# A last batch of graphs: update's start, block sums and message additions put in another order

## The chip, the cores and the metric

The kernel runs on one core of one Trainium2 chip. The time is device microseconds of that core, as the median of several runs. It was 2236.86 us before the change (three runs, 2236.06 to 2238.81). A profiled execution of 2235.71 us, with a span of 2233.9 us, gives the trace.

## The reference

There are 64 graphs of 256 nodes with 256 features each (fp32), and a 256 x 256 adjacency per graph. Two layers follow one another:

```python
# layer 0, per graph
h = relu(bn(conv1(x)));  x_conv = relu(bn(conv2_17taps(h)) + x)
s = x @ w_se.T + b_se                         # 3 numbers per node
A = exp(-(|s_n|^2 + |s_m|^2 - 2 s_n.s_m)) * adj
x_nmp = A @ relu(x @ w_msg.T + b_msg)
gi = concat(x_conv, x_nmp) @ w_ih.T + b_ih;  gh = x @ w_hh.T + b_hh
r = sigmoid(gi_r + gh_r);  z = sigmoid(gi_z + gh_z)
n = tanh(gi_n + r * gh_n)
x = layernorm(x + (1 - z) * n + z * x)
# layer 1
h = layernorm(x)
x = layernorm(x + x + relu((adj @ h) @ W_rel + b_rel + h @ W_root))
```

## The kernel before, in words

The graphs are worked in eight batches of eight. The 17-tap convolution of a batch is computed for the batch ahead, in a transformed form, while the graphs of the present batch go through the gates. In the last batch (`first_k` = 56 to graph 62) no convolution is left to run beside them, so that batch has a loop of its own (L1246 to L1277). Graph 63 is done by `last_graph`.

Every engine works its instructions in the order in which the program issues them; `manual_schedule` keeps that order for all five. So the order of the calls in the loop is the order on each engine. Several functions are generators: each `step(...)` issues the instructions up to the next `yield`. A pass of graph k works on five graphs at once:

- `load(k + 3)`, `load_x(k + 1)`: SP's DMAs of the transposed x, the adjacency and x.
- `block_gates(k)`, four steps (`ga`): the gates of graph k as a block product with seven products of left and right sums, TensorE (PE) into four PSUM banks `ps_a`, `ps_d`, `ps_b`, `ps_c`. VectorE (DVE) adds each product into its place in `XF` (`onto`, L831). The third step accumulates a further product into `ps_a` with `start=False`; it may start only when DVE has read the first product there. The fourth step makes the n part of `gh` (`ps_n`, L856; DVE's addition at L858).
- `block_sums(k + 1, i)`: four DVE additions (L808 to L811) that make left sums of one input of the next graph: i = 0 its transposed x, 1 its message result (`NMP`), 2 its convolution (`xc`).
- `passing(k + 1)`: PE's product of masked weights and messages; ACT copies it to `NMP` (L738).
- `factors(k + 2)`, `distances(k + 2)`, `mask(k + 2)`: the exponentials and the masking of a graph's weights. `distances` has four small PE matmuls (L724) and two exponentials on ACT (L726); `mask` is one DVE product (L729).
- `messages(k + 3)`, two steps (`msg`): PE's product into `ps_msg` (L678); then DVE's additions (L688 and L690 twice), ACT's relu (L692) and five small GpSimd (POOL) operations (L696 to L700).
- `update(k)`, three steps (`up`): first two DVE operations on `nn` and tanh on ACT (L873); then `w` (L877 to L879), its statistics (L864, L865 twice), and on POOL the powers for the layer norms (L886 to L888) and a shift (L890, L891); then `h` on DVE (L896) and x1 on ACT (L899).
- `transposes_h(k - 1)`, `project(k - 1)`, `aggregate(k - 1)`: layer 1 of the graph before: PE's transposes (L909), ACT's `hT` (L911), PE's product with both weights (L922), ACT's copies of one half to `hr` (L923), PE's product with the adjacency (L934), DVE's `y` (L936, L938), its statistics, POOL's powers, and ACT's last scaling (L950) with the output DMA (L951).

One place of `block_gates`, in its third step:

```python
t = product(a, 5, False)
onto(0, 1, t, 1)
onto(1, 0, t, 0)
onto(0, 1, product(b_, 2, False))
squash(0)
```

Of the kernel before, what the change touches and what calls it, by code (L numbers as in the profile page):

```python
# [17 lines left out]
B, N, D = 64, 256, 256  # L18
# [58 lines left out]
def gnn_two_layers(  # L77
# [22 lines left out]
    def bank(name):  # L100
        return psum.tile([P, 512], F32, tag="ps", name=name)
# [548 lines left out]
    def load(k):  # L650

        if k >= B:
            return
        load_xt(k)
        load_adj(k)
# [9 lines left out]
    def load_x(k):  # L665
        if k < B:
            XG[k] = work.tile([P, C, D], F32, tag="x", name="x")
            nc.sync.dma_start(out=XG[k], in_=x[k].rearrange("(c p) d -> p c d", p=P))
# [39 lines left out]
    def factors(k):  # L708
        st, ns = ST[k]
        ps = bank("ps_sT")  # L710
        for m in range(C):
            nc.tensor.transpose(ps[:ROWS, m * P:(m + 1) * P], st[:, m, :ROWS], ident)
        lr = ahead.tile([ROWS, 2, N], F32, tag="lr", name="lr", bufs=1)
        nc.scalar.activation(lr[:, 0, :], ps[:ROWS, :N], AF.Identity, bias=lone[:, 1:2], scale=lone[:, 0:1])
        nc.scalar.copy(lr[:, 1, :], ps[:ROWS, :N])
        ST[k] = (lr, ns)

    def distances(k):
        lr, ns = ST[k]
        AT[k] = ahead.tile([P, C, N], F32, tag="AT", name="AT", bufs=2)  # L720
        pss = [bank("ps_dist") for _ in range(C)]
        for m in range(C):
            r = slice(m * SR, m * SR + 4)
            nc.tensor.matmul(pss[m][:, :N], lr[r, 0, m * P:(m + 1) * P], lr[r, 1, :], start=True, stop=True)  # L724
        for m in range(C):
            nc.scalar.activation(AT[k][:, m, :], pss[m][:, :N], AF.Exp, bias=ns[:, m:m + 1], scale=2.0)  # L726

    def mask(k):
        nc.vector.tensor_mul(AT[k], AT[k], ADJ[k])  # L729

    def passing(k):
        NMP[k] = work.tile([P, C, N], F32, tag="nmp", name="nmp")
        ps = bank("ps_nmp")
        for d in range(C):
            for m in range(C):
                nc.tensor.matmul(ps[:, d * N:(d + 1) * N], MSG[k][:, m, d * P:(d + 1) * P], AT[k][:, m, :],  # L736
                                 start=(m == 0), stop=(m == C - 1))
        nc.scalar.copy(NMP[k].rearrange("p c n -> p (c n)"), ps)  # L738
# [59 lines left out]
    def block_sums(k, i):  # L798

        if i == 2:  # L800
            xc, g = XC[k]
            v = xc[:, :, g, :]
        else:
            v = (XT, NMP)[i][k]
        a11, a12, a21, a22 = (v[:, c, n * P:(n + 1) * P] for n in range(C) for c in range(C))
        at = S * D + ((k % 2) * 3 + i) * 4 * P
        s1, s2, s3, s4 = (XF[:, at + j * P:at + (j + 1) * P] for j in range(4))
        nc.vector.tensor_add(s1, a21, a22)  # L808
        nc.vector.tensor_sub(s2, s1, a11)
        nc.vector.tensor_sub(s3, a11, a21)  # L810
        nc.vector.tensor_sub(s4, a12, s2)  # L811
        LEFT[k, i] = (a11, a12, s4, a22, s1, s2, s3)
# [54 lines left out]
    def update(k):  # L867

        rz, gn = RZ[k]
        nn = work.tile([P, C, D], F32, tag="nn", name="nn", bufs=1)  # L870
        stt(nn, rz[:, :, :D], 1.0, gn[:, :, D:], op0=ALU.add, op1=ALU.mult)
        stt(nn, nn, 0.5, gn[:, :, :D])
        nc.scalar.activation(nn, nn, AF.Tanh)  # L873
        yield

        w = work.tile([P, C, D], F32, tag="w", name="w", bufs=1)
        nc.vector.tensor_sub(w, XG[k], nn)  # L877
        stt(w, rz[:, :, D:], 3.0, w, op0=ALU.add, op1=ALU.mult)
        stt(w, nn, 4.0, w)  # L879
        mv = work.tile([P, C, 2], F32, tag="mv", name="mv", bufs=4)  # L880
        for n in range(C):
            stats(mv, n, w[:, n, :])


        q = work.tile([P, 2, C], F32, tag="q", name="q", bufs=4)
        nc.gpsimd.tensor_scalar(q[:, 0, :], mv[:, :, 1], 4 * EPS, None, ALU.add)  # L886
        nc.gpsimd.tensor_scalar(q[:, 1, :], mv[:, :, 1], 1 + EPS, 4 * EPS * EPS, ALU.mult, ALU.add)
        nc.gpsimd.tensor_tensor(q, q, mhalf[:, :2 * C].rearrange("p (a c) -> p a c", a=2), ALU.pow)  # L888
        sh = work.tile([P, C], F32, tag="sh", name="sh", bufs=4)
        nc.gpsimd.tensor_mul(sh, mv[:, :, 0], q[:, 0, :])  # L890
        nc.gpsimd.tensor_scalar(sh, sh, -1.0, None, ALU.mult)  # L891
        yield
        H[k] = work.tile([P, C, D], F32, tag="h", name="h", bufs=1)
        X1[k] = work.tile([P, C, D], F32, tag="x1", name="x1", bufs=2)
        for n in range(C):
            nc.vector.tensor_scalar(H[k][:, n, :], w[:, n, :], mv[:, n, 0:1], q[:, 1, n:n + 1],  # L896
                                    ALU.subtract, ALU.mult)
        for n in range(C):
            nc.scalar.activation(X1[k][:, n, :], w[:, n, :], AF.Identity, bias=sh[:, n:n + 1], scale=q[:, 0, n:n + 1])  # L899
        yield  # L900


    def transposes_h(k):
        hT = work.tile([P, C, N], F32, tag="hT", name="hT", bufs=1)
        ps = bank("ps_hT")
        for c in range(C):
            for n in range(C):
                q = c * N + n * P
                nc.tensor.transpose(ps[:, q:q + P], H[k][:, n, c * P:(c + 1) * P], ident)  # L909
        for c in range(C):  # L910
            nc.scalar.activation(hT[:, c, :], ps[:, c * N:(c + 1) * N], AF.Identity,  # L911
                                 bias=gb[:, 1, c:c + 1], scale=gb[:, 0, c:c + 1])
        H[k] = hT

    def project(k):
        hT = H[k]
        hr = work.tile([P, C, D], F32, tag="hr", name="hr", bufs=1)
        outs = []
        for n in range(C):
            ps = bank("ps_out")  # L920
            for c in range(C):
                nc.tensor.matmul(ps, hT[:, c, n * P:(n + 1) * P], wrr[:, c, :], start=(c == 0), stop=(c == C - 1))  # L922
            nc.scalar.copy(hr[:, n, :], ps[:, :D])  # L923
            outs.append(ps)
        OUTS[k] = (hr, outs)
# [29 lines left out]
    def step(g):  # L955
        if g is not None:
            next(g, None)
# [218 lines left out]
    for b in range(NB):  # L1176
# [19 lines left out]
        for k in range(b * BG, min((b + 1) * BG, B - 1)):  # L1196
            load(k + 3)
            load_x(k + 1)
            up = update(k)
# [46 lines left out]
    for k in range(first_k, B - 1):  # L1246
        load(k + 3)
        load_x(k + 1)
        ga, up = block_gates(k), update(k)
        step(ga)  # L1250
        step(y_left)
        step(ga)
        transposes_h(k - 1)
        step(ga)
        passing(k + 1)
        if k + 2 < B:
            factors(k + 2)
            block_sums(k + 1, 0)
            block_sums(k + 1, 2)
        step(ga)  # L1260
        project(k - 1)
        if k + 2 < B:
            distances(k + 2)
        msg = messages(k + 3) if k + 3 < B else None
        step(msg)
        step(up)
        step(msg)
        step(up)
        if k + 2 < B:
            block_sums(k + 1, 1)  # L1270
        step(up)
        if k + 2 < B:
            mask(k + 2)
        agg = aggregate(k - 1)
        step(agg)
        step(agg)
        y_left = agg  # L1277
# [44 lines left out]
```

## Time and profile before

| | before |
|---|---|
| time, median (three runs) | 2236.86 us (2236.06 to 2238.81) |
| span of the profiled execution | 2233.9 us |
| busy: PE, DVE, ACT, POOL | 2201.5, 1720.5, 773.3, 531.9 us |
| a pass of the last batch (graphs 56 to 60) | 25.17 to 25.19 us |
| granted TensorE clock in these passes | 1.00 |

The profile counts an engine as busy while it executes an instruction; waiting and issuing DMAs is not busy. A timeline line has the start in us from the span's start, the length in us, the engine, the line of the kernel, the operation, what is written and read, and in brackets the idle time before it with the instruction that ended it. A line of the waits has the waiting instruction, the one that it waited for, the total in us, how often, and the longest. A pass of the last batch is 25.2 us long, so the whole loop of seven graphs is under a tenth of the span.

### The profile page before, as it was taken

The page shows a single profiled execution, that of the slowest core. Times are in us where ns is not written, and L with a number is a line of the kernel's source. Part 1 is how long each engine was busy: PE and PEld are TensorE (multiplying, and loading weights), DVE is VectorE, ACT ScalarE, POOL GpSimd, SP SyncE. Part 2 cuts the span into 40 slices and gives each one's busy share as a digit, 9 for nine tenths or more (in the row PEclk, how much of TensorE's full clock was granted, in tenths as well). Part 3 has the DMA queues.
Part 4 walks back from the last instruction along what each step waited for, and adds up shares of the span by engine and source line. Part 5 has one row for each costly group of instructions (what it writes and reads, how often), then busy time and mean ns, then how long its engine had stood idle before and what let it go on. Part 6 is the DMA issues. An engine that isn't in the chain of part 4 may idle for free.

```text
span 2233.9 us, 24739 instructions
## 1 busy us (share of the span) xinstructions
PE 2201.5 (99%) x8400; PEld 1460.0 (65%) x8400; DVE 1720.5 (77%) x3322; ACT 773.3 (35%) x1594; POOL 531.9 (24%) x933
## 2 busy tenths in 40 slices
PE   8999999999999999999999999999999999999998
PEld 5776676666765676656766567666676667666664
DVE  6967989398873998749886598957989388896665
ACT  6533323532244322433224422243222532234333
POOL 0112222132122321223122231223222132121222
PEclk9999999999999999999999999999999999999999
DMA  5932442314323152233422243231442214421100
GB/s 149 316 117 67 141 137 76 104 38 150 123 76 109 52 177 78 76 104 108 146 81 81 80 132 123 76 99 67 141 128 85 95 47 140 134 71 43 43 29 19
DMA packets 212683, 226.70 MB, mean 101 GB/s; under 512 B 22103, under 2 KB 203854, under 8 KB 212558
## 3 DMA queue, kind: packets, MB, share of 16 engines
q1 hardware_dynamic: 190128, 191.27, 27.1%
q10 hardware_dynamic: 22430, 33.86, 4.4%
q8 instruction: 67, 1.10, 0.2%
q14 instruction: 58, 0.48, 0.1%
HBM read 179.22 MB, written 45.88 MB: 101 GB/s over the span
## 4 chain that ended last, share of the span: by engine, by line
PE 73%; DVE 19%; DMA 3%; issue 2%; POOL 2%; ACT 1%; SPq 0%; POOLq 0%; DVEq 0%; ACTq 0%
PE ps_k L386 13%; PE ps_rz L755 12%; PE ps_out L922 8%; DVE XF L104 6%; PE ps_rz L752 6%; PE ps_n L767 6%; PE ps_c L492 5%; PE ps_msg L678 4%; PE ps_nmp L736 4%; PE ps_n L765 3%; DMA w<-w2m 2%; PE ps_out L934 2%; PE ps_w L230 2%; DVE XF L456 2%; DVE bst L864 2%
## 5 line engine op out<-in xcount | busy, mean ns | idle before, releaser
L104 DVE SCALAR_TENSOR_TENSOR XF<-XF 128x512 f32<-128x512 f32 (+2 forms) x800 | 507.9, 666 | 7.4
L386 PE MATMUL ps_k<-w,XF 128*128 128x256 f32 x1316 | 294.7, 381 | 6.1 <-DMA w<-w2m 4.5
L696 POOL TENSOR_TENSOR sq<-st 128x6 f32<-128x6 f32 x64 | 13.7, 214 | 1128.0 <-DVE st L688 1079.1
L386 PEld LDWEIGHTS ps_k<-w,XF 128*128 128x128 f32 x1316 | 247.9, 190 | 47.7 <-issue 4.9
L922 PE MATMUL ps_out<-wrr,hT 128*128 128x512 f32 x504 | 226.7, 592 | 0.1
L759 ACT ACTIVATE rz<-rz 128x512 f32<-128x512 f32 x114 | 71.9, 631 | 444.4 <-DVE rz L758 444.4
L899 ACT ACTIVATE x<-w,sh,q 128x256 f32<-128x256 f32 x126 | 68.8, 593 | 424.6 <-POOL sh L891 424.6
L752 PE MATMUL ps_rz<-whh,xT 128*128 128x512 f32 x456 | 214.8, 593 | 0.0
L755 PE MATMUL ps_rz<-wih,nmp 128*128 128x512 f32 x456 | 214.3, 592 | 0.0
L755 PE MATMUL ps_rz<-wih,xc 128*128 128x512 f32 x456 | 214.3, 592 | 0.0
L768 DVE TENSOR_TENSOR gn<-ps_n,brzn 128x512 f32<-128x512 f32 x114 | 78.2, 686 | 170.2 <-PE ps_n L767 170.2
L755 PEld LDWEIGHTS ps_rz<-wih,xc 128*128 128x128 f32 x456 | 86.6, 190 | 109.1 <-issue 109.1
L755 PEld LDWEIGHTS ps_rz<-wih,nmp 128*128 128x128 f32 x456 | 86.6, 190 | 109.1 <-issue 109.1
L922 PEld LDWEIGHTS ps_out<-wrr,hT 128*128 128x128 f32 x504 | 95.2, 190 | 93.8 <-issue 81.8
L758 DVE TENSOR_TENSOR rz<-ps_rz,brzn 128x512 f32<-128x512 f32 x114 | 77.6, 681 | 76.3 <-PE ps_rz L755 76.2
L678 PE MATMUL ps_msg<-wms,xT 128*128 128x260 f32 x512 | 129.9, 396 | 0.0
L362 DVE TENSOR_TENSOR XF<-XF 128x512 f32<-128x512 f32 (+3 forms) x128 | 126.2, 1010 | 1.7
L736 PE MATMUL ps_nmp<-AT,msg 128*128 128x256 f32 x512 | 121.0, 379 | 0.0
L752 PEld LDWEIGHTS ps_rz<-whh,xT 128*128 128x128 f32 x456 | 82.1, 190 | 58.3 <-issue 55.0
L934 PE MATMUL ps_out<-hr,adj 128*128 128x256 f32 x504 | 119.5, 380 | 0.0
L492 PE MATMUL ps_c<-xTc,w 128*128 128x512 f32 x256 | 115.4, 593 | 3.0 <-ACT xTc L482 3.0
L765 PE MATMUL ps_n<-whh,xT 128*128 128x256 f32 x456 | 117.2, 379 | 0.0
(200 smaller groups left out, 3763.9 us busy)
## 6 DMA issues: line engine op xcount, KB each, us to landing
w<-w2m SPq DMA_DIRECT2D x105, 768.0 KB, 5.5
xn<-in_x_dram SPq DMA_DIRECT2D x32, 512.0 KB, 4.3
xt<-xTc ACTq DMA_DIRECT2D x32, 512.0 KB, 3.2
xT<-xt SPq DMA_DIRECT2D x64, 256.0 KB, 3.0
xb<-in_x_dram SPq DMA_DIRECT2D x32, 512.0 KB, 5.4
adj<-in_adjT_dram SPq DMA_DIRECT2D x64, 256.0 KB, 2.7
x<-in_x_dram SPq DMA_DIRECT2D x64, 256.0 KB, 3.0
out_dram<-y ACTq DMA_DIRECT2D x63, 256.0 KB, 2.2
```

What stands on the lines that cost most here:

```text
L104: nc.vector.scalar_tensor_tensor(o, in0, s, in1, op0=op0, op1=op1)
L362: (nc.vector.tensor_add if add else nc.vector.tensor_sub)(sl(o, n), sl(a, n), sl(b, n))
L386: nc.tensor.matmul(ps, X[:, slot, c * P:(c + 1) * P], w(m, c), start=first and c == 0, stop=(c == C - 1), skip_group_check=True)
L492: nc.tensor.matmul(pss[o], w1[:, c, o * P:(o + 1) * P], xTc[:, c, :], start=(c == 0), stop=(c == C - 1))
L678: nc.tensor.matmul(ps[:, :D + 4], XT[k][:, c, m * P:(m + 1) * P], wms[:, c, :], start=(c == 0), stop=(c == C - 1 and not idle))
L736: nc.tensor.matmul(ps[:, d * N:(d + 1) * N], MSG[k][:, m, d * P:(d + 1) * P], AT[k][:, m, :], start=(m == 0), stop=(m == C - 1))
L752: nc.tensor.matmul(prz, XT[k][:, c, q], whh[:, c, 0:2 * D], start=(c == 0), stop=False)
L755: nc.tensor.matmul(prz, ins[i], wih[:, i, 0:2 * D], start=False, stop=(j == 3))
L765: nc.tensor.matmul(pn[:, D:], XT[k][:, c, q], whh[:, c, 2 * D:], start=(c == 0), stop=(c == C - 1))
L767: nc.tensor.matmul(pn[:, :D], t, wih[:, i, 2 * D:], start=(i == 0), stop=(i == 3))
L922: nc.tensor.matmul(ps, hT[:, c, n * P:(n + 1) * P], wrr[:, c, :], start=(c == 0), stop=(c == C - 1))
L934: nc.tensor.matmul(po, ADJ[k][:, m, n * P:(n + 1) * P], hr[:, m, :], start=False, stop=(m == C - 1), skip_group_check=True)
```

## The change

Only the order of calls in the last batch's loop changes. `update`'s first step (the two operations on `nn` and the tanh) is issued ahead of `project`. The block sums of the next graph's message result are issued ahead of `distances`. `update`'s second step (`w`, its statistics, the powers) is issued ahead of the messages' second step (their additions, relu and small POOL operations). No instruction is added or taken away.

```diff
@@ -1258,16 +1258,15 @@
             block_sums(k + 1, 0)
             block_sums(k + 1, 2)
         step(ga)
+        step(up)
         project(k - 1)
         if k + 2 < B:
+            block_sums(k + 1, 1)
             distances(k + 2)
         msg = messages(k + 3) if k + 3 < B else None
         step(msg)
         step(up)
         step(msg)
-        step(up)
-        if k + 2 < B:
-            block_sums(k + 1, 1)
         step(up)
         if k + 2 < B:
             mask(k + 2)
```

## What I predict

> **What bounds the kernel now.** I read the page's first part, then the busy time by stretches of the last batch (graphs 56 to 62, the loop that the change edits), then the waits of the matrix engine there, then the timeline of one pass. The page:
>
> ```profile
> PE 2201.5 (99%) x8400; PEld 1460.0 (65%) x8400; DVE 1720.5 (77%) x3322; ACT 773.3 (35%) x1594; POOL 531.9 (24%) x933
> ```
>
> PE (TensorE) is busy 99% of the span, so anything that PE waits for costs time, and nothing else does. Three passes of the last batch, cut where the second product into `ps_a` starts (columns: stretch, length, busy time with instruction counts, granted clock, DMA):
>
> ```profile
> 2059.53:2084.70 25.17, 24.17 (x92) 16.33 (x92) 17.24 (x45) 8.49 (x17) 5.70 (x15) 1.00 0.12 42
> 2084.70:2109.89 25.19, 24.18 (x93) 16.34 (x93) 17.24 (x45) 8.49 (x17) 5.71 (x15) 1.00 0.13 43
> 2160.24:2184.43 24.19, 22.42 (x84) 14.81 (x84) 16.34 (x41) 7.86 (x16) 3.32 (x10) 1.00 0.08 22
> ```
>
> PE is idle 1.00 us of each ordinary pass and 1.77 us of the pass of graph 61, which has no messages left to make. VectorE (DVE) is busy only 17 of 25 us: it has time to spare, but in the wrong place. The waits of PE from 2009 us to the end name one cause:
>
> ```profile
> PE ps_a L826 <- DVE XF L831: 8.6, 7, 1.8
> PE ps_hT L1006 <- DVE h L997: 0.6, 1, 0.6
> ```
>
> Seven waits: 1.81 (in graph 56's gates), five of 1.00 or 1.01, and 1.78 us (graph 62's). PE wants to add the next product into `ps_a`, and may not before DVE has read the first one there (`onto`, L831). The restart shows in the timeline of PE:
>
> ```profile
> 2083.10 0.60 PE L909 MATMUL ps_hT<-ident,h 128*128 128x128 f32 x4
> 2084.70 1.99 PE L826 MATMUL ps_a<-wsum,XF 128*128 128x256 f32 x6 [1.01 <-DVE XF L831]
> 2086.53 0.59 PE L826 MATMUL ps_b<-whh,XF 128*128 128x256 f32 x2
> ```
>
> The wait is longer than the record says. Where nothing is waited for, the work after these four transposes starts 0.44 us after them (2206.35 to 2206.79); here it is 1.60 us. And the six matmuls into `ps_a` take 1.83 us to the next group, where the six into `ps_b` take 1.72 (2061.35 to 2063.07). So one wait costs 1.16 + 0.11 = 1.27 us of PE.
>
> Why DVE is late, from its timeline in the same pass (times from the span's start, length, idle time before in brackets):
>
> ```profile
> 2070.19 0.69 DVE L104 SCALAR_TENSOR_TENSOR nn<-nn,XF 128x512 f32<-128x512 f32 x1
> 2073.81 0.17 DVE L688 TENSOR_TENSOR st<-ps_msg,bms 128x6 f32<-128x6 f32 x1 [2.93 <-PE ps_msg L678]
> ...
> 2075.10 0.68 DVE L877 TENSOR_TENSOR w<-x,nn 128x512 f32<-128x512 f32 x1
> ...
> 2078.26 0.18 DVE L865 BATCH_NORM_AGGREGATE mv<-bst 128x2 f32<-128x6 f32 x1
> 2078.36 0.26 DVE L808 TENSOR_TENSOR XF<-nmp 128x128 f32<-128x128 f32 x1
> ...
> 2080.27 0.73 DVE L896 TENSOR_SCALAR h<-w,mv,q 128x256 f32<-128x256 f32 x2 [0.93 <-POOL q L888]
> ...
> 2084.12 0.53 DVE L831 TENSOR_TENSOR XF<-ps_a,brzn 128x384 f32<-128x384 f32 x1
> ```
>
> DVE finishes `nn` at 2070.88 and stands for 2.93 us until the message product is there. Only then come `w`, its statistics, GpSimd's (POOL) powers, `h`, the mask, `y`, its statistics, and at the end of that line the read of `ps_a` that PE wants.
>
> [...]the power at L888 took 1.16 us beside the block sums and 1.02 us in graph 62, where DVE stood still. [...]here tanh follows exp at 2073.46 with no gap, so another order of the two should load no table.
>
> **The change, part by part** (times of the same pass; each part on the clock that PE sets, since up to `nn` DVE follows PE).
>
> Tanh of `nn` goes ahead of `project`. The two DVE steps ahead of it are where they were (DVE had nothing else to do). On ACT the tanh (0.63 us) now stands before the two `hr` copies instead of after the exponentials: from 2070.92 to 2071.55. The first copy was at 2070.39 and moves to about 2071.5; the second waits for PE until 2072.11 in any case. The aggregation (L934, 2074.49) needs both and doesn't notice: cost nothing, hidden by the second half of the projection. In graph 62 tanh would run from 2195.60 to 2196.23 and the first copy end at about 2196.55, 0.24 us before the second can start (2196.79): also nothing, though tight.
>
> Block sums of the message result (four adds, 0.98 us from 2078.36 to 2079.34) move into DVE's 2.93 us of idle time: 2070.91 to 2071.89. Their input, `nmp`, was copied by 2067.30. They leave a place in which they lay inside POOL's 1.80 us: neither price shows on the path, but they delay `w` by 0.35 us beyond tanh.
>
> `w` ahead of the messages' additions: `w` starts at 2071.9, when tanh is there, instead of 2075.10. From there to the last statistic it takes 3.34 us (2075.10 to 2078.44): 2075.24. POOL then needs 1.80 (2078.44 to 2080.24) for the powers: 2077.04. Meanwhile DVE does the four additions of the messages, 2 x 0.49 = 0.98 us, all of it inside POOL's time. `h` starts at 2077.07 instead of 2080.27: 3.20 us earlier. `h` to the end of the first `onto` is 4.38 us (2080.27 to 2084.65), none of it waiting for PE: the aggregation that `y` reads was over at 2076.38. So `ps_a` is free at 2081.45, and PE gets there at 2083.54: 2.1 us of slack, the wait is gone.
>
> Graph 61: `nn` ends at 2171.60, block sums at 2172.60, `w` there instead of at 2174.83, so `h` and all behind it come 2.23 us earlier; the first `onto` ends at 2182.16 instead of 2184.39, PE arrives at 2182.06 + 0.44 = 2182.50. Slack 0.34 us, gone too. Its cost now: 2184.43 - 2182.50 + 0.11 = 2.04 us.
>
> What waits longer: the messages' results come about 0.9 us later (2076.2 instead of 2075.18), and POOL makes their five small operations behind the powers, not ahead, done at about 2080.3 instead of 2077.62. They are read by `factors` in the next pass, near 2091.5: nothing. The messages' PSUM buffers are free 0.9 us later; PE opens none of them before the transposes at 2083. SP's and ACT's DMAs keep their place: `x` for the next graph is behind `adj` (2076.41, behind the aggregation), so a `w` done earlier doesn't call it earlier.
>
> The sum: the first of the seven waits comes from the pass of graph 55, which is not edited. Five at 1.27 are 6.35, one at 2.04: 8.4 us; I take 8.3, since single restarts differ by 0.01 to 0.02. The profiled span of 2233.9 becomes 2225.6. After graph 62 PE works without a gap but the copy's to 2212, and DVE is waiting for PE there (3.87 us at 2212.14), so the tail moves along whole and no more. The profiled run took 2235.71, the others 2236.06 to 2238.81: I take 8.3 off the median of 2236.86, which gives 2228.6. A bound from below: the recorded idle time alone, 5.02 + 1.78 = 6.8, which gives 2230.1. From above: POOL's powers, no longer beside the block sums, gain at most 0.14 a pass, in slack; so 8.4 and the scatter of the runs, some 2 us.
>
> **The rivals.**
> *Another wait takes its place, partly.* PE's next needs are `hT` and `squash`, both already served by ACT in time[...]. The 2.1 us of slack in five passes speak against it. If half of the gain goes, 4.1 us are left: 2232.7, within 0.2% (4.5 us, about what a measurement here can tell from no change). Chance 0.08.
> *The clock pays it back.* A fuller PE might be granted less. For 8.3 us in the 150 us of these passes 5.5% would be needed; the clock in all rows above is 1.00 at 24.17 of 25.17 us. 2236.9; chance 0.01.
> *Slower: tanh blocks ACT.* Tanh now stands ahead of the copies that the aggregation on PE needs. It is free until tanh ends at 2073.55 (two copies of 0.37 less overlap before L934 at 2074.27); worked out is 2071.55. Every pass is slower than before once tanh ends 2.0 + 1.27 = 3.3 us late, by a DVE that brings `nn` so late. At 4.3 us late, 1 us a pass and six passes: 2242.9. DVE's idle 2.93 us right after `nn` speaks against it. Chance 0.03.
> *The edit doesn't do what it says.* The generators are stepped by hand; `update`'s first step ends at its tanh, so they agree. 2236.9, chance 0.01.
>
> **How the numbers follow.** Likeliest (0.87): 2228.6. Range 2226.3 to 2232.4: below, the scatter of the runs around the full sum; above, the recorded idle time alone (2230.1) plus the same scatter. Faster by over 0.2%: 0.88 (with a part of the first rival), same 0.09, slower 0.03.
>
> **What would show it.** Passes of 23.9 us for graphs 56 to 60 in place of 25.18; no wait of PE at `ps_a` but the first, of 1.81; DVE's 2.93 us of idle time behind `nn` filled by L808 to L811 and `w`; L690 beside POOL's L888; the first `onto` some 2 us before PE's product. It is wrong if PE waits at L934 for `hr`, or at L826 with DVE still late, or if the passes stay above 25 us.

## The result, and the profile after

The changed kernel takes 2225.76 us (median of four runs, 2224.53 to 2226.82), beside 2236.46 us before (four runs, 2233.51 to 2238.81). The ratio is 0.9953, with a 95% interval of 0.9935 to 0.9970: faster. I had predicted 2228.6 us, and a range of 2226.3 to 2232.4, whose lower end is 0.5 us above the measured median. The profiled spans are 2233.9 and 2223.2 us, 10.7 us apart, where my sum had 8.3.

The page of the changed kernel first. TensorE (PE) does the same work:

```profile
span 2223.2 us, 24736 instructions
...
PE 2199.6 (99%) x8400; PEld 1460.6 (66%) x8400; DVE 1719.7 (77%) x3322; ACT 774.3 (35%) x1594; POOL 529.8 (24%) x933
```

Passes of the last batch, cut at the same place as before (stretch, length, then busy time and instructions of PE, weight loads, DVE, ACT and POOL, the granted clock and the DMA). In each, PE is now busy for the whole of it; an ordinary pass has gone from 25.17 to 23.90 us, that of graph 61 from 24.19 to 22.16:

```profile
2055.99:2079.89 23.90, 23.90 (x94) 16.30 (x93) 17.05 (x46) 8.51 (x18) 5.16 (x14) 1.00 0.14 45
2079.89:2103.80 23.91, 23.91 (x95) 16.31 (x93) 17.07 (x46) 8.50 (x18) 5.16 (x14) 1.00 0.14 44
...
2151.61:2173.77 22.16, 22.16 (x87) 14.79 (x86) 15.54 (x41) 6.80 (x15) 2.76 (x7) 1.00 0.08 24
```

The waits of PE to the end: of seven at `ps_a`, the one that comes from the unedited pass of graph 55 is left. The second line belongs to `last_graph` and is the same as before.

```profile
PE ps_a L826 <- DVE XF L831: 1.8, 1, 1.8
PE ps_hT L1006 <- DVE h L997: 0.6, 1, 0.6
```

The timeline of PE has the product into `ps_a` 0.43 us behind the transposes, where it was 1.60, and 1.73 us ahead of the next group, where it was 1.83:

```profile
2079.46 0.60 PE L909 MATMUL ps_hT<-ident,h 128*128 128x128 f32 x4
2079.89 1.89 PE L826 MATMUL ps_a<-wsum,XF 128*128 128x256 f32 x6
2081.62 0.59 PE L826 MATMUL ps_b<-whh,XF 128*128 128x256 f32 x2
```

And the timeline of VectorE (DVE) in one pass (that of graph 56), the same operations as shown of before:

```profile
2042.64 0.69 DVE L104 SCALAR_TENSOR_TENSOR nn<-nn,XF 128x512 f32<-128x512 f32 x1
2043.26 0.28 DVE L808 TENSOR_TENSOR XF<-nmp 128x128 f32<-128x128 f32 x1
...
2044.19 0.69 DVE L877 TENSOR_TENSOR w<-x,nn 128x512 f32<-128x512 f32 x1
...
2047.35 0.18 DVE L865 BATCH_NORM_AGGREGATE mv<-bst 128x2 f32<-128x6 f32 x1
2047.45 0.13 DVE L688 TENSOR_TENSOR st<-ps_msg,bms 128x6 f32<-128x6 f32 x1
...
2049.24 0.74 DVE L896 TENSOR_SCALAR h<-w,mv,q 128x256 f32<-128x256 f32 x2 [0.93 <-POOL q L888]
...
2053.09 0.53 DVE L831 TENSOR_TENSOR XF<-ps_a,brzn 128x384 f32<-128x384 f32 x1
```

DVE no longer stands behind `nn`; the messages' additions lie beside POOL's powers (2047.62 to 2049.21); the first read of `ps_a` ends at 2053.62, and PE comes for it at 2055.99.

**Where the 10.7 us are.** The edited instructions begin after the first wait in graph 56. In the profile of before PE ends that wait at 2034.35 us, in that of the change at 2031.98: 2.37 us are there already, ahead of anything that was edited. From that place to the end it is 199.55 us before and 191.17 after: 8.38 us. So two questions are left: is it the mechanism of my sum that gave the 8.38, and what are the 2.37?

### The profile page after: what moved, and what is told of

Its sections match the earlier page's. It is cut to its first block, busy times and chain, and to the rows that moved or that the text cites. A ratio compares the mean times of both kernels' runs of the same rounds, so it can differ in the third digit from the quotient of the medians.

```text
span 2223.2 us, 24736 instructions
## 1 busy us (share of the span) xinstructions
PE 2199.6 (99%) x8400; PEld 1460.6 (66%) x8400; DVE 1719.7 (77%) x3322; ACT 774.3 (35%) x1594; POOL 529.8 (24%) x933
## 4 chain that ended last, share of the span: by engine, by line
PE 74%; DVE 19%; issue 2%; DMA 2%; POOL 1%; ACT 1%; SPq 0%; POOLq 0%; DVEq 0%; ACTq 0%
PE ps_k L386 13%; PE ps_rz L755 11%; PE ps_out L922 7%; DVE XF L104 7%; PE ps_rz L752 6%; PE ps_n L767 6%; PE ps_c L492 5%; PE ps_msg L678 4%; PE ps_nmp L736 4%; PE ps_n L765 3%; PE ps_out L934 3%; PE ps_w L230 2%; DVE XF L456 2%; PE ps_dist L724 1%; DMA w<-w2m 1%
## 5 line engine op out<-in xcount | busy, mean ns | idle before, releaser
L934 PE MATMUL ps_out<-hr,adj 128*128 128x256 f32 x504 | 119.6, 380 | 0.0
```

The lines of the kernel that those rows point to most:

```text
L934: nc.tensor.matmul(po, ADJ[k][:, m, n * P:(n + 1) * P], hr[:, m, :], start=False, stop=(m == C - 1), skip_group_check=True)
```

## The experiments

In the table, "ahead" is where PE ends the wait at `ps_a` in graph 56 (from its timeline), and "behind" is the span, to 0.01 us, less that. The time is the median of the runs of that kernel; its ratio to the kernel before has its 95% interval. The first two lines ran beside each other, four runs each. The kernels from "tanh alone" to "no block sums" ran beside a set of 38 runs of the kernel before (median 2235.2 us), the others beside a set of 33 (median 2235.08 us).

| kernel | ahead | behind | time | ratio |
|---|---|---|---|---|
| before, first profile | 2034.35 | 199.55 | 2236.46 | 1 |
| changed, first profile | 2031.98 | 191.17 | 2225.76 | 0.9953 (0.9935 to 0.9970) |
| tanh alone | 2034.87 | 197.52 | 2232.02 | 0.9987 (0.9978 to 0.9996) |
| additions alone | 2033.14 | 194.05 | 2229.67 | 0.9975 (0.9965 to 0.9984) |
| no additions | 2033.87 | 196.93 | 2232.86 | 0.9991 (0.9984 to 0.9998) |
| no block sums | 2032.95 | 191.16 | 2225.93 | 0.9963 (0.9950 to 0.9976) |
| changed, again | 2032.64 | 191.15 | 2226.62 | 0.9964 (0.9951 to 0.9976) |
| before, again | 2032.60 | 199.56 | 2233.95 | 1.0000 (0.9991 to 1.0008) |
| five subtractions | 2029.52 | 197.04 | 2233.02 | 0.9993 (0.9986 to 1.0000) |
| graph 55 too | (2030.79, no wait) | 191.05 | 2223.63 | 0.9954 (0.9941 to 0.9966) |

**Tanh alone.**

```diff
         step(ga)
+        step(up)
         project(k - 1)
 ...
         step(msg)
-        step(up)
         step(msg)
         step(up)
```

> The order of before, with update's first step (nn, tanh) ahead of the projection and nothing else. My theory: in graphs 56 to 60 the message additions still stand ahead of w on VectorE and wait for TensorE's message product, so w starts at the same place and the wait of 1.00 us at ps_a stays in five passes (25.18 us each); only graph 61, which has no messages, loses its wait. From the first wait at ps_a in graph 56 to the end: 2.0 us less than before (199.5 us), not 8.3. Rival (tanh on ScalarE was what held w): the passes of 56 to 60 get shorter too, by 1.2 us each. For the unedited part ahead of that wait (2034.35 us in the profile of before, 2031.98 in that of the change): if it scatters from run to run it lies anywhere from 2031 to 2036; if the new order reaches into it, it stays at 2032.

Behind the first wait 2.03 us are gained, as expected. The five passes are 25.17 to 25.19 us still, with waits of 1.00 and 1.01; that of graph 61 is 22.25 and has none. The timeline of DVE shows why an early tanh is worth nothing where there are messages: their additions stand in the way of `w` and wait for PE.

```profile
2074.33 0.17 DVE L688 TENSOR_TENSOR st<-ps_msg,bms 128x6 f32<-128x6 f32 x1 [2.92 <-PE ps_msg L678]
...
2075.21 0.17 DVE L688 TENSOR_TENSOR st<-ps_msg,bms 128x6 f32<-128x6 f32 x1 [0.38 <-PE ps_msg L678]
...
2075.62 0.68 DVE L877 TENSOR_TENSOR w<-x,nn 128x512 f32<-128x512 f32 x1
```

The rival, that tanh's place on ScalarE held `w`, falls for these passes, and holds for graph 61.

**Additions alone.**

```diff
         step(msg)
         step(up)
-        step(msg)
         step(up)
+        step(msg)
         if k + 2 < B:
             block_sums(k + 1, 1)
```

> The order of before, with the messages' additions behind w and nothing else: tanh still behind the exponentials, block sums still behind w. My theory: w starts when tanh ends, 2074.1 instead of 2075.1 in the pass of graph 57, so the first read of ps_a ends about 1.0 us earlier, at 2083.65, and TensorE, there at 2083.54, still waits 0.1 to 0.2 us: five passes of 24.0 to 24.2 us, 5 to 6 us gained, and graph 61's wait of 1.78 us stays. Rival (all three moves are needed, since four block sums and four additions no longer fit into GpSimd's 1.8 us together): h comes late by 0.2 us or more and the gain is 4 us or less.

The five passes are 24.07 to 24.08 us and 5.50 us are gained; graph 61's wait of 1.78 stays. DVE, after an idle time for tanh, in that kernel's timeline:

```profile
2071.80 0.69 DVE L877 TENSOR_TENSOR w<-x,nn 128x512 f32<-128x512 f32 x1 [3.24 <-ACT nn L873]
...
2076.86 0.74 DVE L896 TENSOR_SCALAR h<-w,mv,q 128x256 f32<-128x256 f32 x2
...
2080.71 0.53 DVE L831 TENSOR_TENSOR XF<-ps_a,brzn 128x384 f32<-128x384 f32 x1
```

```profile
2080.78 0.60 PE L909 MATMUL ps_hT<-ident,h 128*128 128x128 f32 x4
2081.29 1.99 PE L826 MATMUL ps_a<-wsum,XF 128*128 128x256 f32 x6
2083.12 0.59 PE L826 MATMUL ps_b<-whh,XF 128*128 128x256 f32 x2
```

The read ends at 2081.24 and PE starts at 2081.29, 0.51 us behind its transposes instead of 0.44, and the group takes 1.83 us again instead of 1.73. The waits view no longer lists these five, and still each pass is 0.17 us longer than in the change. The rival (additions and block sums don't fit into POOL's powers) falls: from the start of the last statistic to that of `h` it is 1.89 us (2074.97 to 2076.86), as in the change (2047.35 to 2049.24), where no block sums lie between them.

**No additions.**

```diff
         step(msg)
-        step(up)
         step(msg)
         step(up)
+        step(up)
```

(against the changed kernel: the additions ahead of `w` again)

> The changed order, with the messages' additions put back ahead of w: tanh and the block sums stay early. My theory: as with tanh alone. VectorE does the block sums in its idle time and then waits for the message product all the same; w starts near 2075.1, the waits of 1.00 us in five passes stay, graph 61's goes: 2.0 us less than before from the first wait at ps_a on. Rival (the block sums were the cost, 0.98 us in front of h): the passes get shorter by up to 1 us each, 5 us in all.

2.62 us are gained, not 2.0. The waits are there, as expected, but of 0.88 to 0.90 us, not 1.00. DVE and POOL in that kernel:

```profile
2073.22 0.16 DVE L688 TENSOR_TENSOR st<-ps_msg,bms 128x6 f32<-128x6 f32 x1 [1.99 <-PE ps_msg L678]
...
2074.51 0.68 DVE L877 TENSOR_TENSOR w<-x,nn 128x512 f32<-128x512 f32 x1
...
2079.57 0.74 DVE L896 TENSOR_SCALAR h<-w,mv,q 128x256 f32<-128x256 f32 x2 [1.72 <-POOL q L888]
```

```profile
2078.49 1.04 POOL L888 TENSOR_TENSOR q<-q,mhalf 128x4 f32<-128x4 f32 x1
```

The power takes 1.04 us where it took 1.16 before. These 0.12 us a pass are the 0.6 us that I missed. It is not enough that block sums lie beside the power: in "additions alone" all four do, and it takes 1.02 us. The traces differ in what starts first. The kernel before, and then "additions alone":

```profile
2079.06 0.28 DVE L811 TENSOR_TENSOR XF<-nmp,XF 128x128 f32<-128x128 f32 x1
2079.08 1.16 POOL L888 TENSOR_TENSOR q<-q,mhalf 128x4 f32<-128x4 f32 x1
```

```profile
2075.80 1.02 POOL L888 TENSOR_TENSOR q<-q,mhalf 128x4 f32<-128x4 f32 x1
2075.85 0.28 DVE L808 TENSOR_TENSOR XF<-nmp 128x128 f32<-128x128 f32 x1
```

Where an addition starts 0.02 us ahead of the power, the power takes 1.15 to 1.16 us; where the first one starts 0.05 us behind it, 1.02 or 1.03. Graph 61 of the kernel before, with no messages' additions, has the first order again (2178.80 and 2178.82), and 1.15 us. No run moved that start alone, so this is read from the traces and not tested. The rival's other size, 1 us a pass for block sums that leave the path, is not there.

**No block sums.**

```diff
         project(k - 1)
         if k + 2 < B:
-            block_sums(k + 1, 1)
             distances(k + 2)
 ...
         step(msg)
+        if k + 2 < B:
+            block_sums(k + 1, 1)
         step(up)
```

(against the changed kernel)

> The changed order, with the block sums of the message result put back behind w and the additions: tanh early, additions behind w. My theory: w starts when tanh ends, some 0.3 us earlier than in the change; the block sums and the additions together (1.9 us) fill GpSimd's 1.8 us and push h back by 0.1 to 0.2 us; the slack of 2.3 us in front of TensorE takes that, so all six waits are gone and the time is that of the change within 0.3 us (8.3 us less than before). Rival (the block sums had to leave their place): waits come back, passes above 24.2 us.

191.16 us behind the first wait, against 191.17 of the change: nothing is lost. `w` starts 0.70 us behind the end of `nn` instead of 0.86, and `h` 5.75 us behind it instead of 5.91. The block sums' early place takes 0.16 us of slack and gives nothing here. I had expected `h` to be pushed back; the eight operations just fit (1.89 us from the last statistic to `h`, as in the change).

**The kernels again, unaltered.**

> The changed kernel once more, unaltered. Two theories of the 2.4 us by which the changed profile was ahead at the first wait in graph 56, before any edited instruction. Scatter of the stretches with the convolution: the start of that wait lies anywhere from 2031 to 2036 us here, and the ratio of times comes nearer to 8.3/2236, 0.9963. Systematic (the new order, or where its instructions lie, quickens the unedited part): it lies at 2032 within 0.5 us again, and the ratio stays near 0.9952. From that wait to the end: 191.2 us in both.

> The kernel before once more, unaltered, as the counterpart. Scatter: the first wait in graph 56 starts anywhere from 2031 to 2036 us. Systematic: at 2034.4 within 0.5 us. From that wait to the end 199.5 us in both, and a ratio of 1.000 within 0.001.

Behind the first wait both repeat to 0.02 us: 191.15 and 199.56. Ahead of it they do not: 2032.64 and 2032.60, now with the two orders alike. Over the nine profiles whose instructions are unedited up to there, that place lies between 2029.52 and 2034.87, and the earliest belongs to "five subtractions", which keeps only 2.5 us of the gain. The systematic theory falls. The two later sets ran on two different chips, and on the first the place lies later (2032.95 to 2034.87) than on the second (2029.52 to 2032.64); but the kernel before has the same median on both, within 0.12 us, so the chip does not show in the time. The ratio, with 33 runs of the kernel before, is 0.9964; 8.38 us less is 0.9963.

**Five subtractions.**

```diff
-        nc.vector.tensor_sub(w, XG[k], nn)
+        for _ in range(5 if k >= (NB - 1) * BG else 1):
+            nc.vector.tensor_sub(w, XG[k], nn)
```

(against the changed kernel)

> The changed kernel, with the subtraction at L877 done five times instead of once in graphs 56 to 62 (the result is the same): 4 x 0.72 = 2.88 us more in front of h on VectorE. In the changed profile the first read of ps_a ends 2.37 us before TensorE wants it (2053.62 against 2055.99), and 0.62 us in graph 61 (2173.15 against 2173.77). My theory (TensorE waits for nothing else, and the slack is what the timeline says): the wait comes back with about 0.6 us of lost time in five passes and 2.4 us in graph 61, 5.4 us in all: passes of 24.5 us. Rival (something else than this read set the passes before): other passes than that, or a wait elsewhere.

The waits are back, seven of them:

```profile
PE ps_a L826 <- DVE XF L831: 6.1, 7, 2.2
```

The ordinary passes are 24.59 to 24.60 us, 0.69 us more, and that of graph 61 is 24.59 instead of 22.16, 2.43 more; 5.87 us in all, with 5.4 expected. 2.88 us of added work let PE start 1.02 us behind its transposes instead of 0.44; so the slack of an ordinary pass was 2.88 - 0.58 = 2.3 us, where the timeline had 2.37. The group behind the wait, 1.83 us again instead of 1.73, makes the 0.58 up to nearly 0.69. Beside these, no wait came up that the changed kernel lacks.

**Graph 55 too.**

```diff
+            last = k == (NB - 1) * BG - 1
+            if last:
+                step(up)
             if k > 0:
                 project(k - 1)
 ...
             step(msg)
             step(up)
             step(msg)
             pump()
-            step(up)
+            if not last:
+                step(up)
             pump()
```

(against the changed kernel, in the loop of the earlier batches)

> The changed kernel, with the same order in the pass ahead of the last batch, that of graph 55, whose late h causes the one wait that is left at ps_a (1.82 us in graph 56): update's first step ahead of the projection, w ahead of the messages' additions. My theory: w of graph 55 starts about 3.5 us earlier, the wait goes, and with the restart 2.1 us are gained over the change: from the start of the last transposes before that place to the end 2.1 us less. Rival (the pass of graph 55 is held by the convolution's last work on ScalarE and VectorE too): the wait shrinks by less than 1 us or moves to another place.

From the start of the projection of graph 54, PE's last work ahead of this edit, to the end: 208.19 us in the changed kernel (again), 206.12 here, so 2.07 us are gained. No wait at `ps_a` is left. PE's timeline at the place:

```profile
2030.35 0.60 PE L909 MATMUL ps_hT<-ident,h 128*128 128x128 f32 x4
2030.79 1.89 PE L826 MATMUL ps_a<-wsum,XF 128*128 128x256 f32 x6
```

It has the lowest median of these kernels: 2223.63 us, beside 2226.62 for the change, with five runs each; of these 3.0 us the edited stretch accounts for 2.07.

## Why the prediction was right, and where it was wrong

*What bounds, and the waits.* Right. PE's wait for the first read of `ps_a` was the cost, and the timeline's 1.27 us for one such wait, not the recorded 1.00, was the price: an ordinary pass lost 25.17 - 23.90 = 1.27 us. Graph 61 was put at 2.04 us and gave 24.19 - 22.16 = 2.03.

*The sum.* 8.4 us worked out, 8.3 taken; 8.38 us measured from the first wait to the end.

*Tanh ahead of the copies to `hr`.* Free, as predicted: it ran at 2043.37, the first copy at 2043.91 and the second at 2044.55, when PE had its half ready; no wait at L934 came up. That tanh and exp in another order load no table held too: the trace of either kernel has one ACT_TABLE_LOAD in the whole span, of 1.28 us at L482. The early tanh is what frees graph 61 (2.03 us alone), and in the other passes it makes the slack: "additions alone", without it, has none, and "no block sums", with it, has all of the gain.

*Block sums.* I priced their move at nothing on the path and a delay of `w` by 0.35 us; it was 0.16, at no gain. "No block sums" has the full gain.

*Additions behind `w`.* This is the part that counts: 5.50 us of 8.38 alone, and without it five of six waits stay. One slip of the working: the messages' results come 2076.2 - 2075.18 = 1.0 us later, not the 0.9 that I wrote. Nothing hung on it.

*The slack.* 2.1 us worked out, 2.37 read from the changed timeline; 0.34 and 0.62 in graph 61. I had kept POOL's 1.80 us for the powers, and they took 1.68. I had put the power's 1.16 us, against 1.02 where DVE stood still, down to the block sums beside it. That was too simple: the 1.16 us of before against 1.04 in "no additions" fit it, but beside the same block sums the power took 1.02 us in "additions alone". The runs show when the power was slow, not why.

*The rivals.* None took place: the clock stayed at 1.00 in passes in which PE is never idle, and neither ACT nor another wait stepped in.

*The failed step* is the base from which the gain was taken: "I take 8.3 off the median of 2236.86", with "the scatter of the runs, some 2 us" below. The mechanism and the gain were right. Three runs gave that median; in two later sets of 38 and 33 runs the kernel before has 2235.2 and 2235.08 us, and goes from 2232.16 to 2239.78. My starting point was 1.7 to 1.8 us too high, and the room that I gave for such a thing too small; the profiled run's 2235.71 was at hand, and nearer. From 2235.1 the sum gives 2226.7. The rest is scatter of the first four runs of the changed kernel: they have 2225.76, the five later ones 2226.62, all nine together 2226.58. The 2.37 us between the first two profiles were 0.04 us between the second two, so nothing shows a part of the edit in them.

*What stays open.* What makes the stretches with the convolution scatter by 5 us was not settled. One piece shows in the profiles, the waits of PE for filter data:

```profile
PE ps_k L386 <- DMA w<-w2m: 4.5, 9, 0.9
```

That is the kernel before; the changed one has 2.5 us in 7 waits. But before (again) has 4.4 us there and reaches the last batch about as early as the change does, so it is not the whole. In "additions alone" other waits of the same products, for DVE, add up to 3.4 us.

Another piece is the granted clock. From 1990 to 1998 us it is 0.79 in "tanh alone", and likewise in "no additions", where the kernel before has 1.00; "no block sums" has 0.79 from 18 to 26 us. The mean over the profiled run is 0.998 in these three, and 0.999 or 1.000 in the other seven. "Tanh alone", then the kernel before (columns as above):

```profile
1990.00:1998.00 8.00, 7.44 (x30) 6.01 (x31) 7.76 (x14) 3.15 (x8) 3.18 (x5) 0.79 0.37 115
```

```profile
1990.00:1998.00 8.00, 6.72 (x32) 5.03 (x33) 7.79 (x14) 3.85 (x10) 2.67 (x5) 1.00 0.29 83
```

By an estimate from these figures, 0.21 of 8 us, up to 1.7 us are lost there, in two of the profiles that reach the last batch late. But the kernel before reaches it late without that. How these pieces come about was not tested.

## What to carry to other kernels

Where the busiest engine stops at a regular place, follow the engine that it waits for back to its own idle time: an operation issued early in an in-order queue, but waiting for a late product (here the messages' additions, for which DVE stood 2.92 us in "tanh alone"), holds back everything behind it, and the cure is to put it behind what is ready. Price a wait from start to start against a place where nothing waits, since the recorded idle time leaves out the restart (here 1.00 us recorded, 1.27 lost). And for a gain of a few tenths of a per cent, a few runs' median is no firm base: compare the edited stretch in both traces, and let the range take in the scatter of the rest.

## What the runs showed of the hardware

A small GpSimd power over 128 x 4 numbers took 1.15 to 1.16 us where a DVE addition of 128 x 128 numbers (L811) had started 0.02 us ahead of it. With four such additions beside it, the first of them 0.05 us behind its start, it took 1.02 or 1.03 us, and with none beside it 1.02 to 1.04. A stopped PE lost 0.10 us more in the group behind a wait (1.83 against 1.73 us), beyond the 0.16 us by which the recorded idle time (1.00) falls short of the delay (1.16). A wait as short as in "additions alone" cost 0.17 us a pass without showing in the waits at all.
